# Moving strip copies ahead of the reading, a tanh between ScalarE's two gelu steps, and two bias additions from GpSimd to VectorE

## The chip, the cores and the metric

The kernel runs on one core of one Trainium2 chip. A core has five engines with an instruction stream each: TensorE (PE; its weight loads are listed as PEld), VectorE (DVE), ScalarE (ACT), GpSimd (POOL) and SyncE (SP), which issues most of the DMAs. [...] The metric is the device time of one execution in microseconds (us); a profiled execution has a span, from its first to its last recorded event, inside its own time.

## The reference, cut to what matters

`x` is 3327 x 64, `adj` a 3327 x 3327 matrix of zeros and ones, about 16 neighbours per row. Two layers follow each other, each added to `x`:

```
h = relu(layernorm(x))
x_t     = logmap0(h)                                   # c = 1 / r**2
adj_att = sigmoid(left[:, None] + right[None, :] + b) * adj
support = sum_j adj_att[i, j] * logmap(h[i], h[j])
x = x + proj(expmap(h, support))

h = relu(layernorm(x))
s = h @ weight
rank = cumsum(adj != 0, axis=1);  deg = rank[:, -1:];  k = min(deg, 100)
w = mask * where(rank - (deg - k) > 0, 0.5 ** (deg - rank), 0)
x = x + w @ s + bias
```

The first layer needs, for each pair of nodes, a function of three inner products; the second weights each neighbour by a power of two that depends on how many neighbours come behind it in its row.

## The kernel before, in words

**Tiling.** The nodes are padded to 26 blocks of 128. The columns i of the transposed `adj` are cut into four strips of 8, 8, 6 and 4 blocks (`STRIPS`); inside a strip the blocks j are taken from the last to the first. One *round* is one j in strips 0 to 2 and two j in strip 3, so that a tile is 128 x 1024, or 128 x 768 in strip 2. There are R = 91 rounds: 0 to 25, 26 to 51, 52 to 77 and 78 to 90. `js(n)` lists a round's blocks.

**One round.** For round n:

- `load` (L617): SyncE brings the 512 or 384 KB of `ad`, four rounds ahead, into one of five buffers.
- `edges` (L623): VectorE makes the 0/1 `mask`, two rounds ahead.
- `count` (L634, L635): TensorE counts neighbours behind each place into `pc`, of which there is one; one round ahead.
- `read` (L652 on ScalarE, L654 or L656 on VectorE): brings `pc` into the 8-bit or 16-bit store `behind`. `ON_ACT` says which share of the reads is ScalarE's: 1 of 2, 5 of 8, 3 of 4 and 1 of 2 by strip. The next `count` has to wait for it. In strip 3 a round has two counts and two reads, and the first read is VectorE's, the second ScalarE's.
- `products` (L680, L681): TensorE puts the pair's inner products in `pq`, one of two buffers in PSUM.
- `gelus` (L873, L874): ScalarE turns `pq` in place by two steps, the second of which takes what the first has written.
- `sigmoids` (L663): ScalarE writes tanh of the two nodes' logits into `sg`, one of five buffers, one round ahead; two instructions in strip 3.
- `pair_one` (L668): VectorE multiplies `sg` and `ad`.
- `pair_two` (L673): VectorE multiplies the result with `pq`, which is free then for the products two rounds on.
- `total` (L693): TensorE sums `sg` over j into the strip's two PSUM banks `po`, two rounds later.

**The order** on TensorE, VectorE and ScalarE is the program's (`manual_schedule(engines=IN_ORDER)`): the loop over n at L1244 writes it out by hand. GpSimd's and SyncE's order is the scheduler's. In the steady state of strips 0 to 2, ScalarE's order in round n is first step, second step, tanh of n+1, read (where it is ScalarE's); VectorE's is `pair_one(n)`, mask of n+2, read (where it is VectorE's), `pair_two(n)`; TensorE's is `total(n-2)`, count of n+1, products of n+1.

**The handover between strips.** Two rounds after a strip's last one, `strip_out` (L1170) copies the strip's sums out of `po`, the first 512 columns by VectorE (L1175), the rest by ScalarE (L1177). A round later `turn` (L1182) has TensorE transpose the copy (L1187) into the same banks, and `per_node` (L1190) copies that (L1197, L1199) and starts `post`: 64 features per node, for which VectorE does twelve larger operations, one per round in strips 1 and 2 and up to two per `advance` in strip 3, and GpSimd many small ones.

**The end.** With the last strip's sums the second layer starts: `decode` makes 16-bit weights of `behind` (L1336, L1339, L1340), `add` multiplies them with `s2` (L1237), and for each of four groups `copied` (L1378 to L1382) and `close` (L1384) bring the sums through one more matmul (L1390) and an addition with `x_sb` (L1392) to the output. `bias` (L1350) has GpSimd add the bias into `x_sb`, six times; two of these, for blocks 16 to 21 and 22 to 25, stand behind `finish()` in the program (L1366, L1367), and GpSimd ran them when `x_sb` was no longer needed unbiased, at 347.45 and 376.74.

Of the kernel before, what the change touches and what calls it, by code (L numbers as in the profile page):

```python
# [18 lines left out]
AF = mybir.ActivationFunctionType  # L19
# [4 lines left out]
P = 128  # L24
N = 3327
NB = 26
NP = NB * P
D = 64
K = D + 2
STRIPS = [(0, 8), (8, 8), (16, 6), (22, 4)]  # L30
# [42 lines left out]
QS = ZS * ZS / 2  # L73
WB = 936.0 / QS
WG = 4.885261340725196
WH = -0.0959413860521814
# [373 lines left out]
def fast(ctx, tc, x, adj_t, r, w_att, b_att, weight, bias, out, flag):  # L450

    nc = tc.nc
    V, A, G, T = nc.vector, nc.scalar, nc.gpsimd, nc.tensor
# [106 lines left out]
    R = len(rounds)  # L560
# [7 lines left out]
    ad_of, mask_of, sg_of, pq_of = {}, {}, {}, {}  # L568
# [31 lines left out]
    def part(n, t, j, a=0, b=None):  # L600
        k, lo, hi = rounds[n]
        F = strips[k].F
        return t[:, (j - lo) * F + a : (j - lo) * F + (F if b is None else b)]

    def span(n):
        k, lo, hi = rounds[n]
        return (hi - lo) * strips[k].F

    def js(n):
        k, lo, hi = rounds[n]  # L610
        return range(hi - 1, lo - 1, -1)
# [46 lines left out]
    def sigmoids(n):  # L658

        S = strips[rounds[n][0]]  # L660
        sg_of[n] = sg = work.tile([P, FMAX], F32, name="sg", bufs=SGB)
        for j in js(n):
            A.activation(part(n, sg, j), S.left[:, : S.F], AF.Tanh, bias=right[:, j : j + 1], scale=0.5)  # L663
# [62 lines left out]
    for hs in node_halves:  # L726
        n = hs.stop - hs.start
# [132 lines left out]
    bias_b = across(bias, D, "bias_b")  # L860
# [7 lines left out]
    A.copy(nz[:, high, 0], zf[:, high])  # L868
    V.tensor_copy(nu[:, high, :D], zf[:, high])

    def gelus(n):
        pq = pq_of[n][:, : span(n)]
        A.activation(pq, pq, AF.Gelu, scale=-WG / QS)  # L873
        A.activation(pq, pq, AF.Gelu, scale=WH)  # L874

    def logits(bs, plr=None):

# [28 lines left out]
    for b in (24, 20, 16, 12, 8, 4, 0):  # L906
        n = min(4, NB - b)
# [262 lines left out]
    def strip_out(k):  # L1170
        S = strips[k]
        S.ot = work.tile([P, FMAX], F32, name="sg", bufs=SGB)[: D + 1]
        for po, (f0, f1) in zip(S.po, S.hv):
            if f0 == 0:
                V.tensor_copy(S.ot[:, f0:f1], po[: D + 1, : f1 - f0])  # L1175
            else:
                A.copy(S.ot[:, f0:f1], po[: D + 1, : f1 - f0])  # L1177
# [49 lines left out]
    late = STRIPS[-1][0]  # L1227
# [16 lines left out]
    for n in range(2, R):  # L1244
        k, lo, hi = rounds[n]
        m, w = n + AHEAD, span(n)
        ended, turned = (n > i and rounds[n - i - 1][1] == 0 for i in (1, 2))
        if n + LOADS < R:
            if rounds[n + LOADS][2] == NB:
                strip_in(rounds[n + LOADS][0])  # L1250
            load(n + LOADS)
        fresh = EARLY <= m < R
        two = fresh and len(js(m)) == 2
        if two:
            count(m, js(m)[0])
        apart = k + 1 == len(STRIPS)
        if turned and not apart:
            pa = turn(k - 1)
        if n >= 4 and (apart or not turned):
            total(n - 2)  # L1260
        gelus(n)
        asked_of_act()
        if turned and not apart:
            finish()
            stages.append(Stage(per_node(k - 1, pa)))
        pair_one(n)
        if two:
            read(m, js(m)[0])
        if EARLY <= m + 1 < R:
            edges(m + 1)  # L1270
        if n == 2:
            for j in js(2):
                read(2, j, True)
        if n < 4:
            products(n + 1)
        if n == 2:
            total(1)
        if fresh:
            count(m, js(m)[-1])
        if n + 1 < R:  # L1280
            sigmoids(n + 1)
        if fresh:
            read(m, js(m)[-1])
        if 4 <= n < R - 1:
            products(n + 1)
        if ended:
            strip_out(k - 1)
        if hi - lo > 1:
            advance(PORTIONS[k])
        if turned and apart:  # L1290
            pa = turn(k - 1)
        pair_two(n)
        if turned and apart:
            finish()
            stages.append(Stage(per_node(k - 1, pa)))
        if n < 4:
            next(rest_of_ahead)
            continue
        advance(PORTIONS[k])
        if turned and not apart:  # L1300
            total(n - 2)
        if n >= R - len(JD):
            if n == R - len(JD):
                pw[0] = bank(0)
            add(JD[n - R], behind(JD[n - R]), 0)
        if n > R - 3:
            next(range_end)
# [15 lines left out]
    with tc.tile_pool(name="l1", bufs=2, reuse_waits="tile") as l1, tc.manual_schedule(engines=IN_ORDER):  # L1323
        decoded = 0

        def decode(j):

            nonlocal decoded
            if j in JD:
                return behind(j)  # L1330
            spare = decoded % (7 + len(JD)) - 7
            wt = weight_of[:, spare] if spare >= 0 else l1.tile([P, NP], U16, name="wt", bufs=7)
            decoded += 1
            to = by_parity(wt)
            if decoded * ACT_DECODES[0] % ACT_DECODES[1] < ACT_DECODES[0]:
                A.activation(to, behind(j).rearrange("p (k r) -> p r k", r=2), AF.Copy, scale=128.0)  # L1336
            else:
                pairs_of = behind(j).bitcast(U16)
                V.tensor_scalar(to[:, 0], pairs_of, 0xFF, 7, op0=ALU.bitwise_and, op1=ALU.logical_shift_left)  # L1339
                V.tensor_scalar(to[:, 1], pairs_of, 0xFF00, 1, op0=ALU.bitwise_and, op1=ALU.logical_shift_right)  # L1340
            return wt

        every = [*order, *range(late, NB)]
        weights = {j: decode(j) for j in every[: len(JD) + 1]}
        stages.append(Stage(per_node(len(STRIPS) - 1, pa)))
        pw[6] = ps.tile([P, FMAX], F32, name="pc")
        for n, j in beside:
            add(j, behind(j), n)

        def bias(b0, nb):  # L1350
            xb = x_sb[:, b0 : b0 + nb]
            G.tensor_add(xb, xb, bias_b[:, None, :].to_broadcast([P, nb, D]))  # L1352

        for i, j in enumerate(order):
            for jn in every[: i + 1 + LEAD]:
                if jn not in weights:
                    weights[jn] = decode(jn)
            asked_of_act()
            advance(LAST)
            for n in range(len(chunks)):  # L1360
                if j not in JD or n > 4:
                    add(j, weights[j], n)
            if i % 4 == 3 and i < STRIPS[-2][0]:
                bias(i - 3, 4)
        finish()
        bias(STRIPS[-2][0], late - STRIPS[-2][0])  # L1366
        bias(late, NB - late)  # L1367
        for j in range(late, NB):
            if j not in weights:
                weights[j] = decode(j)  # L1370
        kept_of = [l1.tile([P, min(NP - 1024 * q, 1024)], F32, name="ow" if q < 3 else "ow_last", bufs=2 if q < 3 else 1)
                   for q in range(4)]

        def copied(n):
            q, r = chunks[n]
            to = kept_of[q].rearrange("p (k r) -> p r k", r=2)
            if r is None:
                V.tensor_copy(to, by_parity(pw[n][:, :256]))  # L1378
            elif r == 0:
                V.tensor_copy(to[:, 0], pw[n])  # L1380
            else:
                A.copy(to[:, 1], pw[n])  # L1382

        def close(q):  # L1384
            for h in range(0, 8 if q < 3 else 2, 4):
                b0 = 8 * q + h
                nb = min(4, NB - b0)
                pc = pw[2 * q + h // 4]
                for b in range(nb):
                    T.matmul(pc[:, b * D : (b + 1) * D], kept_of[q][:, (h + b) * P : (h + b + 1) * P], w2s, start=True, stop=True)  # L1390
                o = l1.tile([P, 4, D], F32, name="o", bufs=4)
                V.tensor_add(o[:, :nb], pc[:, : nb * D].rearrange("p (b d) -> p b d", d=D), x_sb[:, b0 : b0 + nb])  # L1392
                full = nb if b0 + nb < NB else nb - 1
                f0 = b0 * P
                nc.sync.dma_start(out[f0 : f0 + full * P, :].rearrange("(b p) d -> p b d", p=P), o[:, :full])
                if full < nb:
                    nc.scalar.dma_start(out[f0 + full * P : N, :], o[: N - f0 - full * P, full])

        for n in range(len(chunks)):
            for j in range(late, NB):  # L1400
                add(j, weights[j], n)
            copied(n)
            if n > 0 and n % 2 == 0:
                close(n // 2 - 1)
        close(3)
# [52 lines left out]
```

## Time and profile before

| what | value |
|---|---|
| three runs | 404.16 us median (401.86 to 404.4) |
| the profiled execution's own time | 404.32 us |
| its span | 402.6 us, 4731 instructions |
| busy: PE, DVE, ACT, POOL | 355.0, 367.3, 355.3, 118.1 us (88, 91, 88, 29%) |
| L873, first step | 91 times, 958 ns mean; idle of ScalarE before it 1.1 us in all |
| L874, second step | 91 times, 947 ns mean; idle before it 2.9 us |
| L663, tanh | 103 times, 978 ns mean |
| L668 and L673, the two pair steps | 91 times each, 1144 and 1140 ns; VectorE's idle before L673 4.4 us, 3.8 of it for L874 |
| L1175, L1177, copies of the sums | 0.68 and 0.57 us for 512 columns |
| L1352, bias on GpSimd | 6 times, 1443 ns mean |
| waits of TensorE for L1175 | 2.6 us, twice, longest 1.7 |

A line of a timeline has the start in us from the span's start, the duration in us, engine, line, operation, the tiles written and read with their shapes, a count, and in brackets the engine's idle time just before it with the one it waited for. The durations of two neighbours can overlap on one engine: the next instruction starts before the last one's record has ended. So what an instruction costs its engine is read from start to start, and the duration is used for when its result is there.

### The profile page before, as it was taken

What the parts mean: (1) busy time and instruction counts of PE and PEld (TensorE: products, weight loads), DVE (VectorE), ACT (ScalarE), POOL (GpSimd) and SP (SyncE); (2) the same over time, 40 slices, a digit from 0 to 9 for tenths busy, and PEclk for the clock granted to TensorE, in tenths of its full rate; (3) what the DMA queues carried; (4) which work ended last, traced back from release to release, by engine and by line L of the source; (5) the groups of instructions that cost most, each with busy time, mean ns of one, the idle gap of its engine ahead of it and who ended that gap; (6) DMA issues with size and microseconds to landing.
All of it is one profiled execution on the core that took longest, in us unless ns stands there. A gap on an engine that the chain in (4) does not pass through costs nothing.

```text
span 402.6 us, 4731 instructions
## 1 busy us (share of the span) xinstructions
PE 355.0 (88%) x1460; PEld 151.9 (38%) x1460; DVE 367.3 (91%) x563; ACT 355.3 (88%) x407; POOL 118.1 (29%) x240
## 2 busy tenths in 40 slices
PE   0087999999999999999999899999979899999992
PEld 0063333333333333333333444444433233344462
DVE  4989999999999989999999999899999999898941
ACT  3589999999999999999999999999998999869510
POOL 8145200000000053870052052850240767241200
PEclk9999999999999899999999999999999999999997
DMA  7314555454548435553445545544563440000012
GB/s 202 150 42 133 171 157 158 128 165 138 163 139 237 148 106 156 156 157 109 153 116 148 149 120 157 131 134 128 152 188 117 111 152 0 0 2 1 2 42 52
DMA packets 23298, 48.99 MB, mean 122 GB/s; under 512 B 8789, under 2 KB 9245, under 8 KB 23265
## 3 DMA queue, kind: packets, MB, share of 16 engines
q1 hardware_dynamic: 20993, 47.66, 40.3%
q10 hardware_dynamic: 1808, 0.46, 0.6%
q0 software_dynamic: 464, 0.49, 0.5%
q8 instruction: 13, 0.21, 0.2%
q14 instruction: 20, 0.16, 0.1%
HBM read 46.40 MB, written 0.87 MB: 117 GB/s over the span
## 4 chain that ended last, share of the span: by engine, by line
DVE 32%; ACT 32%; PE 19%; issue 12%; DMA 1%; POOL 1%; POOLq 0%; DVEq 0%; ACTq 0%
ACT sg L663 11%; ACT pq L873 9%; DVE sg L673 8%; DVE sg L668 7%; PE po L693 7%; ACT behind_lo L652 3%; ACT pq L874 3%; PE pc L635 2%; PE pc L634 2%; PE pq L680 2%; PE pq L681 2%; ACT weight_of L652 2%; DVE behind_hi L656 2%; DVE mask L623 1%; ACT behind_hi L652 1%
## 5 line engine op out<-in xcount | busy, mean ns | idle before, releaser
L693 PE MATMUL po<-sg,hw 128*65 128x512 f32 (+1 forms) x364 | 159.5, 561 | 0.0
L673 DVE SCALAR_TENSOR_TENSOR sg<-pq,sg 128x1024 f32<-128x1024 f32 (+1 forms) x91 | 103.8, 1140 | 4.4 <-ACT pq L874 3.8
L668 DVE SCALAR_TENSOR_TENSOR sg<-sg,ad 128x1024 f32<-128x1024 f32 (+1 forms) x91 | 104.1, 1144 | 0.2
L663 ACT ACTIVATE sg<-left_b,right 128x1024 f32<-128x1024 f32 (+2 forms) x103 | 99.5, 978 | 0.0
L874 ACT ACTIVATE pq<-pq 128x1024 f32<-128x1024 f32 (+1 forms) x91 | 86.2, 947 | 2.9
L873 ACT ACTIVATE pq<-pq 128x1024 f32<-128x1024 f32 (+1 forms) x91 | 87.1, 958 | 1.1 <-PE pq L681 0.9
L693 PEld LDWEIGHTS po<-sg,hw 128*65 128x65 f32 x364 | 49.0, 137 | 67.3 <-issue 53.9
L634 PE MATMUL pc<-mask,ca 128*128 128x512 bf16 (+1 forms) x175 | 64.0, 366 | 10.1 <-ACT behind_hi L652 2.8
L680 PE MATMUL pq<-iu,ju 71*128 71x512 f16 (+1 forms) x182 | 67.5, 371 | 1.6 <-ACT jz L810 1.0
L635 PE MATMUL pc<-mask,cb 128*128 128x512 bf16 (+1 forms) x182 | 65.2, 369 | 1.8 <-ACT behind_lo L652 1.7
L681 PE MATMUL pq<-iz,jz 128*128 128x512 f16 (+1 forms) x182 | 65.9, 369 | 0.0
L623 DVE TENSOR_SCALAR mask<-ad 128x1024 bf16<-128x1024 f32 (+1 forms) x91 | 58.8, 647 | 0.0
L1062 POOL TENSOR_TENSOR dots<-dots,ih 128x8 f32<-128x8 f32 (+1 forms) x3 | 3.1, 1022 | 130.0 <-DVE dots L1082 130.0
L635 PEld LDWEIGHTS <-cb 128*128 128x128 bf16 x182 | 17.8, 98 | 51.8 <-issue 40.3
L634 PEld LDWEIGHTS <-ca 128*128 128x128 bf16 x175 | 17.2, 98 | 29.5 <-issue 17.3
L680 PEld LDWEIGHTS <-ju 71*128 71x128 f16 x182 | 17.9, 99 | 23.1 <-DVE sg L673 5.1
L1237 PEld LDWEIGHTS <-s 128*128 128x128 f16 x182 | 17.7, 98 | 20.2 <-issue 1.5
L681 PEld LDWEIGHTS <-jz 128*128 128x128 f16 x182 | 18.1, 99 | 19.1 <-issue 2.1
L652 ACT ACTIVATE behind_lo<-pc 128x1024 uint8<-128x1024 f32 (+2 forms) x29 | 24.9, 859 | 0.0
L1352 POOL TENSOR_TENSOR x_sb<-x_sb,bias_b 128x256 f32<-128x256 f32 (+1 forms) x6 | 8.6, 1443 | 51.7 <-DVE w L1151 46.0
L652 ACT ACTIVATE behind_hi<-pc 128x1024 uint8<-128x1024 f32 (+2 forms) x25 | 21.8, 871 | 1.2 <-PE pc L635 1.2
L844 PE MATMUL pq<-id,nui 128*71 128x128 f16 x8 | 1.0, 311 | 21.2 <-ACT nzi L818 21.2
(336 smaller groups left out, 396.0 us busy)
## 6 DMA issues: line engine op xcount, KB each, us to landing
ad<-in_adj_t SPq DMA_DIRECT2D x65, 512.0 KB, 3.6
ad<-in_adj_t SPq DMA_DIRECT2D x26, 384.0 KB, 3.1
out<-o SPq DMA_DIRECT2D x6, 128.0 KB, 1.9
left_b<-left_d SPq DMA_DIRECT2D x1, 512.0 KB, 5.0
x_sb<-in_x ACTq DMA_DIRECT2D x1, 416.0 KB, 5.7
x_sb<-in_x SPq DMA_DIRECT2D x1, 416.0 KB
left_b<-left_d SPq DMA_DIRECT2D x1, 384.0 KB
jz<-iz POOLq DMA_DIRECT2D x2, 128.0 KB, 2.6
```

What stands on the lines that cost most here:

```text
L623: V.tensor_scalar(*args, 0.0, None, op0=ALU.not_equal)
L634: T.matmul(S.pc[:, f0:f1], ca, S.before[:, f0:f1], start=False, stop=True, skip_group_check=True)
L635: T.matmul(S.pc[:, f0:f1], cb, now[:, f0:f1], start=S.first, stop=True, skip_group_check=True)
L652: A.activation(kept, of, AF.Relu, scale=128.0 if j in JD else 1.0)
L663: A.activation(part(n, sg, j), S.left[:, : S.F], AF.Tanh, bias=right[:, j : j + 1], scale=0.5)
L668: V.scalar_tensor_tensor(sg, sg, 1.0, ad_of.pop(n)[:, :w], op0=ALU.add, op1=ALU.mult)
L673: V.scalar_tensor_tensor(sg, pq_of.pop(n)[:, :w], WD, sg, op0=ALU.add, op1=ALU.mult)
L680: T.matmul(part(n, pq, j, f0, f1), ju[:KB, j, :], S.iu[:, f0:f1], start=True, stop=False)
L681: T.matmul(part(n, pq, j, f0, f1), jz[:, j, :], S.iz[:, f0:f1], start=False, stop=True)
L693: T.matmul(po[: D + 1, : f1 - f0], hw[:, j, :], part(n, sg_of[n], j, f0, f1), start=j == NB - 1, stop=j == 0)
L873: A.activation(pq, pq, AF.Gelu, scale=-WG / QS)
L874: A.activation(pq, pq, AF.Gelu, scale=WH)
```

## The change

- `gelus` is split into `gelu(n, scale)`. In rounds 4 to 89 (`n >= 4 and n + 1 < R`) the tanh of round n+1 stands between the two steps, rather than behind them; rounds 0 to 3 and the last keep the old order.
- `strip_out` of a finished strip comes before the tanh (where that is still at its old place) and before the round's last `read`, and no longer behind `products`.
- The last two additions of the bias are VectorE's, and stand behind the third of the seven `copied` of the end.

```diff
+    def gelu(n, scale):
+        pq = pq_of[n][:, : span(n)]
+        A.activation(pq, pq, AF.Gelu, scale=scale)
+
     def gelus(n):
-        pq = pq_of[n][:, : span(n)]
-        A.activation(pq, pq, AF.Gelu, scale=-WG / QS)
-        A.activation(pq, pq, AF.Gelu, scale=WH)
+        gelu(n, -WG / QS)
+        gelu(n, WH)
...
-        gelus(n)
+        tanh_first = n >= 4 and n + 1 < R
+        gelu(n, -WG / QS)
+        if tanh_first:
+            sigmoids(n + 1)
+        gelu(n, WH)
         asked_of_act()
...
         if fresh:
             count(m, js(m)[-1])
-        if n + 1 < R:
+        if ended:
+            strip_out(k - 1)
+        if n + 1 < R and not tanh_first:
             sigmoids(n + 1)
         if fresh:
             read(m, js(m)[-1])
         if 4 <= n < R - 1:
             products(n + 1)
-        if ended:
-            strip_out(k - 1)
...
-        def bias(b0, nb):
+        def bias(b0, nb, engine=G):
             xb = x_sb[:, b0 : b0 + nb]
-            G.tensor_add(xb, xb, bias_b[:, None, :].to_broadcast([P, nb, D]))
+            engine.tensor_add(xb, xb, bias_b[:, None, :].to_broadcast([P, nb, D]))
...
         finish()
-        bias(STRIPS[-2][0], late - STRIPS[-2][0])
-        bias(late, NB - late)
...
             copied(n)
+            if n == 2:
+                bias(STRIPS[-2][0], late - STRIPS[-2][0], V)
+                bias(late, NB - late, V)
             if n > 0 and n % 2 == 0:
                 close(n // 2 - 1)
```

## The prediction

> **What bounds the kernel now.** I read the page, then the busy time by stage, then the timelines of ScalarE, VectorE and TensorE side by side, and used the waits to see who is late. By stage (columns: length, then busy time of PE, PEld, DVE, ACT, POOL, granted clock, DMA share, GB/s):
>
> ```profile
> 47.00:127.00 80.00, 79.31 (x274) 29.89 (x273) 79.86 (x90) 79.27 (x81) 0.00 (x0) 1.00 0.52 155
> 127.00:145.00 18.00, 16.32 (x57) 6.32 (x56) 16.15 (x20) 16.70 (x20) 2.37 (x5) 0.91 0.54 156
> 235.00:276.00 41.00, 38.63 (x173) 18.50 (x172) 37.40 (x51) 40.56 (x55) 21.41 (x53) 1.00 0.48 135
> 297.00:326.00 29.00, 25.33 (x93) 9.77 (x91) 28.74 (x37) 27.24 (x40) 8.87 (x21) 1.00 0.45 130
> ```
>
> Strip 0 (to 127) has no slack anywhere: from start to start a round costs TensorE 3.45 us, VectorE 3.44, ScalarE 3.46. In strip 1 (to 223) a round of ScalarE costs 3.58 (two steps 1.97, tanh 1.04, a read 0.91 in five rounds of eight), TensorE's 3.45, and twelve rounds carry 0.6 more of VectorE. Strip 2 to 276 is ScalarE's: 40.56 of 41. From 276 to 326 VectorE never rests. The end of strip 3 is a loop through two engines (below). Strip 2, a round in which VectorE waits:
>
> ```profile
> 262.53 0.81 ACT L873 ACTIVATE pq<-pq 128x768 f32<-128x768 f32 x1
> 263.37 0.80 ACT L874 ACTIVATE pq<-pq 128x768 f32<-128x768 f32 x1
> 264.08 0.93 ACT L663 ACTIVATE sg<-left_b,right 128x768 f32<-128x768 f32 x1
> ...
> 264.20 0.96 DVE L673 SCALAR_TENSOR_TENSOR sg<-pq,sg 128x768 f32<-128x768 f32 x1 [0.75 <-ACT pq L874]
> ```
>
> The first step starts 0.84 before the second, which needs its result; the second starts only 0.71 before the tanh, which needs nothing of it. With 1024 columns the two are 1.05 and 0.92: the dependent pair wastes 0.13 us per round. L673 starts 0.83 after the second step (1.04 at 1024).
>
> **The skill.** "ScalarE: Activation LUTs", What ACT_TABLE_LOAD costs: an ACTIVATE with immediates takes 186 ns + 0.833 ns per column (1.04 and 0.83 us here; trace 1.01 and 0.80), and back-to-back ones overlap by about 93 ns. The trace agrees: 1.01 minus 0.92. It is this overlap that the dependent pair loses, plus 0.04. Alternating gelu and tanh loads no table: the trace's last load is at 21.56. "SBUF — State Buffer", SBUF: two separate sides: VectorE and GpSimd take a shared port pair as a lock, and the loser stands still (shown at the tail below). "TensorE: Matmul & The Clock Gate", What's actually happening: an idle TensorE falls to half clock after an idle window of about 3.4 us. The trace falls after 1.68, so I don't count on when.
>
> **Part 1, tanh between the steps.** By the condition on the round number this holds in rounds 4 to 89, all four strips, not only two; the changed program's order confirms it. Nothing is added; first step to tanh isn't in the old trace, so the gain lies between 0 and 0.13, and I take 0.13, since second step to tanh, the same shapes, is 0.92 everywhere. Two effects: ScalarE gains 0.13 per round, and the second step comes one tanh later (0.83 to 1.22), so L673 can too. VectorE runs in order: behind L673 stand L668, the mask and the read of the next round. Written sooner, a tanh needs its sum buffer sooner, one of five; the sum that frees it ran two rounds before, and at the handover about 0.8 ahead: free. I carry the old starts forward.
>
> - Start. The first step of round 4 is at 47.82; then tanh +0.92, second +1.04 = 49.78, L673 +1.04 = 50.82 against 50.10. VectorE has no gap in strip 0 to give it back: +0.7, also for TensorE, whose products in rounds 9 and 11 already wait for L673.
> - Strip 0 otherwise: TensorE's 3.45 stays. Zero; ScalarE merely moves up against the products (old slack 0.7 to 1.6).
> - Strip 1: VectorE's waits for others in rounds 37 to 39 (0.42, 0.50, 0.42) shrink to about 0.45 in all: -0.9. The rounds after carry an extra operation and are VectorE's: zero.
> - Strip 2: VectorE waits 0.66, 0.77, 0.20, 0.62, 0.75, 0.18, 0.17 between 249 and 276. Rounds 58 to 70 gain 12 x 0.13 = 1.5 (3 x 2.94 + 2.25 = 11.1 per four rounds against 11.66). From 276 on VectorE is full: zero.
> - Strip 3. Two reads per round, one by VectorE ahead of L673:
>
> ```profile
> 334.37 1.01 ACT L873 ACTIVATE pq<-pq 128x1024 f32<-128x1024 f32 x1
> 335.41 1.01 ACT L874 ACTIVATE pq<-pq 128x1024 f32<-128x1024 f32 x1
> 336.33 1.32 ACT L663 ACTIVATE sg<-left_b,right 128x512 f32<-128x512 f32 x2
> 337.56 0.58 ACT L652 ACTIVATE behind_lo<-pc 128x512 uint8<-128x512 f32 x1
> ```
>
> The old loop over two rounds: first step to read 3.19, read to the next-but-one first step through count, sum, count and products 4.29 (from 333.86 to 338.15): 7.48, or 3.74 a round. The 0.13 would make it 7.35. But a new loop opens: first step, tanhs 0.92, second step 1.22, L673 1.04, L668 1.14, VectorE's read 1.14, count 0.74, products 0.43, first step 1.07 = 7.70. That is 3.85 a round, where rounds 82 to 84 ran at 3.47. Its start costs too: round 78's first step is held by products at 298.17, its L673 moves from 300.33 to 301.35, +1.0. Carrying starts through rounds 79 to 90 with the extra operations, L673 of round 90 comes 2.6 later: +2.6 in all.
>
> **Part 2, copies ahead of the reading.** Same copies. VectorE's order changes only between strips 0 and 1, the other handovers having no VectorE read in that round; ScalarE's change at three.
>
> ```profile
> 129.79 1.22 DVE L656 TENSOR_SCALAR behind_hi<-pc 128x1024 uint8<-128x1024 f32 x1
> 130.92 0.68 DVE L1175 COPY sg<-po 65x512 f32<-65x512 f32 x1
> ...
> 130.94 0.57 ACT L1177 COPY sg<-po 65x512 f32<-65x512 f32 x1
> ...
> 131.65 0.81 PE L1187 MATMUL po<-ident,sg 65*128 65x65 f32 x8 [1.68 <-DVE sg L1175]
> 132.26 0.63 PE L634 MATMUL pc<-mask,ca 128*128 128x512 bf16 x1
> ```
>
> VectorE's copy moves up by one read, 1.13; ScalarE's by about as much against the products, having freed time. With the +0.7 in front, the transposes start near 131.2 and TensorE idles 0.7 rather than 1.7. After the old idle, eight matmuls start 0.43 apart instead of 0.216 (granted 0.91 of 18 us, 1.6 lost). Whether an idle of 0.7 costs the clock lies between 0 and 1.6; at 226.6 one of 0.9 cost none, so I take 0. VectorE later waited 1.85 at 143.6 for the count; without it, and with its 0.7 delay, L673 of round 30 comes at 143.5 against 144.76: -1.2 net of the start. If the clock still drops, -0.2. The read waits 0.6 behind the copy; its count is needed only by TensorE's next, which then has that room. Between strips 1 and 2 VectorE is the limit; I give nothing for the copy. Queues: TensorE's order is identical; SP's only swaps four small strip loads by one or two places, far ahead of use.
>
> **Part 3, last biases.** GpSimd drops two, VectorE gains 128x384 and 128x256 (0.48 and 0.34 by L1146's starts), after the third copy near 386. They delay output additions by about 0.5; those feed only stores, and VectorE next waits 1.23 for TensorE at 389: free. If that cover failed, +0.8. Gone is this:
>
> ```profile
> 376.74 1.01 POOL L1352 TENSOR_TENSOR x_sb<-x_sb,bias_b 128x256 f32<-128x256 f32 x1 [5.73 <-DVE w_last L1151]
> ...
> 377.08 1.12 DVE L1340 TENSOR_SCALAR weight_of<-behind_hi 128x1664 uint16<-128x1664 uint16 x1
> ...
> 382.75 0.61 PE L1237 MATMUL po<-weight_of,s 128*128 128x512 bf16 x2 [0.77 <-DVE s L1167]
> ```
>
> L1340 takes 0.59 elsewhere; the 0.53 lies on the path to L1167, for which TensorE waits 0.77: -0.5. Near 347.5 an L673 comes 0.17 late under the other bias: -0.2 (0 if chance). Locks elsewhere fall on other instructions now, up to 0.5 either way.
>
> **Sum.** Handover with start -1.2, strip 1 -0.9, strip 2 -1.5, strip 3 +2.6, tail -0.7: -1.7. The profiled execution took 404.32 (span 402.6 and 1.7 around it), so 402.6; the median of the runs is 404.16, 0.16 lower: **402.5**.
>
> **Rivals.** (a) The new loop of strip 3 doesn't bind (reads land sooner than 0.74): the +2.6 goes and the end gains 0.4: 404.2 - 4.7 = about 399.5. For it: VectorE has 0.35 in hand between 7.70 and the old loop. Against: each leg of 7.70 is a start-to-start from this trace. (b) Slower: the late second step holds L673 wherever a stretch of ScalarE's begins, because the first steps can't move up. Then VectorE loses 0.7 at the start, about 0.7 to 0.9 at each of rounds 29, 37 and 58, and 2.6 in strip 3, 5.8 in all; the tail gives 0.7, the freed 0.13s about 2.4: 404.2 + 2.7 = 406.9. It decides if old distances from products' end to first step, 0.5 to 1.9, shrink by less than about half. Against: that distance is ScalarE's own backlog. (c) The copies don't do what they should: the clock drops again after the transposes, so the handover gives 0.2, and VectorE then takes strip 1's gain: 404.2 - 0.2 - 1.5 + 2.6 - 0.7 = 404.4. For it: the old drop came after an idle of only 1.68.
>
> **Numbers.** As sketched 0.5 (own range 401 to 404), (a) 0.2, (b) 0.15, (c) 0.15. About 1% (4.0 us) is what a measurement here can tell from nothing: below 400.1 needs (a) nearly whole, 0.18; above 408.2 needs (b) with another loss, 0.06; the rest 0.76. The range runs from (a) to short of (b): 399.3 to 406.3.
>
> **What would show it.** First step to tanh 0.92 and tanh to second 1.04; VectorE idle 0.7 before round 4's L673; the transposes' wait under 1 us and 0.216 between matmuls after it; fewer VectorE waits between 249 and 276; rounds 82 to 88 near 3.85 with L673 waiting for the second step; L1340 uniform and no wait over 0.3 at the last L1237. I am wrong if strip 3 runs at 3.7 or less, or if waits for the second step appear throughout strips 0 and 1.

## The result, and the profile after

| | us |
|---|---|
| kernel before | 404.38 median (401.86 to 405.64, 14 runs) |
| kernel after | 404.15 median (403.24 to 405.71, 14 runs) |
| ratio | 1.0001, 95% interval 0.9984 to 1.0018 |
| profiled execution of after | 404.36, span 402.6 (before: 404.32, span 402.6) |

The forecast was 1.7 us less; nothing came. The same stages by busy time in after (columns as in the prediction: length, busy PE, PEld, DVE, ACT, POOL, granted clock, DMA share, GB/s):

```profile
127.00:145.00 18.00, 16.77 (x63) 6.42 (x62) 18.00 (x21) 17.31 (x21) 2.68 (x5) 1.00 0.50 148
235.00:276.00 41.00, 39.79 (x180) 19.13 (x179) 38.17 (x52) 41.00 (x57) 21.80 (x52) 1.00 0.52 145
297.00:326.00 29.00, 24.11 (x87) 9.18 (x86) 27.00 (x35) 26.19 (x39) 8.17 (x19) 1.00 0.40 116
326.00:349.00 23.00, 21.61 (x73) 7.80 (x72) 21.78 (x28) 21.16 (x28) 13.55 (x33) 1.00 0.13 41
```

At the handover (first row) the clock is 1.00 instead of 0.91, and VectorE has no gap. In strip 2 ScalarE is full, with 57 instructions where there were 55 in the same 41 us: it runs faster. In strip 3 (third row) VectorE rests 2.0 of 29 us, where it rested 0.26: a new wait. Two groups of the page name it (busy time and mean ns; then the engine's idle time just before, and what ended most of it). In after both steps stand in one line of the program, L873, and the lines behind it have numbers that are 3 higher than before:

```profile
L873 ACT ACTIVATE pq<-pq 128x1024 f32<-128x1024 f32 (+1 forms) x182 | 174.3, 964 | 5.3 <-PE pq L681 3.7
L673 DVE SCALAR_TENSOR_TENSOR sg<-pq,sg 128x1024 f32<-128x1024 f32 (+1 forms) x91 | 103.6, 1139 | 8.0 <-ACT pq L873 7.5
```

VectorE waits 7.5 us for the steps (3.8 before), and ScalarE 3.7 for the products.

To see where time is won and lost I keep a **ledger**: the start of L673 in each of the 91 rounds, minus its start in the first profile of before, with the difference at round 3 taken out. Rounds 0 to 3 run the old order in both kernels; their difference was 0.45 here, and -0.67 to 1.65 in five further profiles of before, so it varies with the execution. For after:

| stretch | forecast | measured |
|---|---|---|
| start, round 4 | +0.7 | +0.74 |
| handover, round 29 to 30 | -1.9 (-1.2 with the start) | -1.91 |
| strip 1, to round 51 | -0.9 | +0.03 |
| second handover, rounds 52 to 57 | 0 | -0.23 |
| strip 2, to round 77 | -1.5 | -1.08 |
| strip 3, round 78 and to 90 | +2.6 | +1.02 and +1.58 |
| tail | -0.7 | -0.58 |
| sum | -1.7 | -0.45 |

With the 0.45 of the start, the two spans are equal.

### The profile page after: what moved, and what is told of

The parts are those of the page before. It is cut to its first block, busy times and chain, and to the rows that moved or that the text cites. A ratio compares the mean times of both kernels' runs of the same rounds, so it can differ in the third digit from the quotient of the medians.

```text
span 402.6 us, 4731 instructions
## 1 busy us (share of the span) xinstructions
PE 354.4 (88%) x1460; PEld 151.1 (38%) x1460; DVE 367.3 (91%) x565; ACT 351.4 (87%) x407; POOL 117.0 (29%) x238
## 4 chain that ended last, share of the span: by engine, by line
DVE 40%; ACT 28%; PE 18%; issue 11%; DMA 1%; POOL 1%; POOLq 0%; DVEq 0%; ACTq 0%
ACT pq L873 15%; DVE sg L673 11%; DVE sg L668 10%; PE po L693 5%; ACT sg L663 5%; DVE behind_lo L656 4%; PE pq L680 2%; PE pq L681 2%; ACT behind_lo L652 2%; DVE behind_hi L656 2%; PE pc L634 2%; PE pc L635 2%; ACT behind_hi L652 2%; ACT weight_of L652 1%; DMA x_sb<-in_x 1%
## 5 line engine op out<-in xcount | busy, mean ns | idle before, releaser
L873 ACT ACTIVATE pq<-pq 128x1024 f32<-128x1024 f32 (+1 forms) x182 | 174.3, 964 | 5.3 <-PE pq L681 3.7
L693 PE MATMUL po<-sg,hw 128*65 128x512 f32 (+1 forms) x364 | 159.5, 561 | 0.0
L673 DVE SCALAR_TENSOR_TENSOR sg<-pq,sg 128x1024 f32<-128x1024 f32 (+1 forms) x91 | 103.6, 1139 | 8.0 <-ACT pq L873 7.5
L668 DVE SCALAR_TENSOR_TENSOR sg<-sg,ad 128x1024 f32<-128x1024 f32 (+1 forms) x91 | 103.8, 1141 | 0.1
L693 PEld LDWEIGHTS po<-sg,hw 128*65 128x65 f32 x364 | 48.9, 137 | 66.8 <-issue 53.5
L656 DVE TENSOR_SCALAR behind_lo<-pc 128x1024 uint8<-128x1024 f32 (+2 forms) x19 | 19.1, 1005 | 0.0
L1359 POOL TENSOR_TENSOR x_sb<-x_sb,bias_b 128x256 f32<-128x256 f32 x4 | 5.5, 1384 | 37.1 <-DVE w L1154 37.1
```

The costliest lines, as they stand in the source:

```text
L656: V.tensor_scalar(kept, S.pc[:, : S.F], 0.0, None, op0=ALU.max)
L668: V.scalar_tensor_tensor(sg, sg, 1.0, ad_of.pop(n)[:, :w], op0=ALU.add, op1=ALU.mult)
L673: V.scalar_tensor_tensor(sg, pq_of.pop(n)[:, :w], WD, sg, op0=ALU.add, op1=ALU.mult)
L693: T.matmul(po[: D + 1, : f1 - f0], hw[:, j, :], part(n, sg_of[n], j, f0, f1), start=j == NB - 1, stop=j == 0)
L873: A.activation(pq, pq, AF.Gelu, scale=scale)
```

## The experiments

Two theories stood against each other. Mine: the change is a sum of separate effects, a gain at the handover, one in strip 2, a loss where the order sets in and a large one in strip 3, and the missing time is in strip 1. The rival: the effects share one slack, so that parts of the change alone give what the whole gives, or the loss of strip 3 is not the new loop. Every kernel below is after with one edit, but for the repeated profiles. The ledger of all:

| kernel | 4 | 29 | 30 | 40 | 57 | 77 | 78 | 90 |
|---|---|---|---|---|---|---|---|---|
| after | 0.74 | 0.72 | -1.19 | -1.17 | -1.39 | -2.47 | -1.45 | 0.13 |
| after_2 (the same again) | 0.75 | 0.72 | -1.19 | -1.16 | -1.38 | -2.45 | -1.43 | 0.15 |
| bias_only | 0.01 | 0.00 | 0.02 | 0.02 | 0.02 | 0.00 | 0.00 | -0.01 |
| copies_only | 0.00 | 0.02 | -1.92 | -1.35 | -1.59 | -1.33 | -1.33 | -1.34 |
| no_tanh | 0.00 | 0.02 | -1.92 | -1.35 | -1.57 | -1.33 | -0.04 | 0.04 |
| tanh_strip0 | 0.75 | 0.72 | -1.20 | -1.20 | -1.44 | -1.18 | 0.10 | 0.18 |
| tanh_strip1 | 0.00 | 0.63 | -1.31 | -1.81 | -2.06 | -2.28 | -2.28 | -2.30 |
| tanh_strip2 | 0.01 | 0.03 | -1.91 | -1.35 | -1.38 | -2.41 | -2.41 | -2.42 |
| tanh_strip3 | 0.01 | 0.02 | -1.91 | -1.35 | -1.57 | -1.33 | -0.31 | 1.26 |
| tanh_half3 | 0.74 | 0.73 | -1.19 | -1.16 | -1.38 | -2.44 | -2.03 | -0.53 |
| tanh_strips12 | 0.01 | 0.64 | -1.30 | -1.81 | -2.02 | -3.10 | -3.10 | -3.10 |
| tanh_late12 | 0.00 | -0.01 | -1.94 | -1.35 | -1.57 | -2.64 | -2.64 | -2.64 |
| before_2, before_3 | 0.01 | 0.00, 0.03 | 0.02 | 0.01, 0.03 | 0.02, 0.06 | 0.01, 0.07 | 0.01, 0.07 | 0.02, 0.07 |
| before_4 | 0.00 | -0.03 | -1.66 | -1.41 | -1.41 | -1.45 | -0.18 | -0.17 |
| before_5 | 0.00 | 0.04 | -1.66 | -1.32 | -1.29 | -1.28 | -1.28 | -1.28 |
| before_6 | 0.01 | 0.03 | 0.03 | 0.03 | 0.06 | 0.07 | 0.07 | 0.08 |

**Without the tanh order: no_tanh.**

```diff
-        tanh_first = n >= 4 and n + 1 < R
+        tanh_first = n >= 4 and n + 1 < R and False
```

> Copies ahead and VectorE's biases kept, the tanh back behind both steps in all rounds. By the ledger of the two traces (each L673 against its old start) the handover between strips 0 and 1 gave 1.9 and the tail 0.6, and the tanh took 0.7 at the start, gave 1.2 in strip 2 and took 2.6 in strip 3. So this one should be about 2.5 under before: ratio 0.994. Rival: the engines are so balanced that what one stage gives comes back as a wait in the next, and the sum is near 1.000 here too.

402.48 us (22 runs), ratio to before 0.9967 (0.9949 to 0.9984): faster than after (1.0001; the two intervals meet at 0.9984), so the tanh order as a whole loses. It is less than the 0.994 that I expected, and not the rival's 1.000. The 1.3 us at round 78 are no part of the edit; copies_only, which differs only in the biases, hasn't them. They are the half clock of which before_4 tells below.

**The order in one strip at a time: tanh_strip0 to tanh_strip3.** The last condition of the same line is `k == 0`, `k == 1`, `k == 2` or `k == 3`.

> As no_tanh, with the tanh between the steps in strip 0 alone (rounds 4 to 25). Ledger: +0.7 at round 4 that VectorE and TensorE carry to the handover; there VectorE waits for TensorE, whose own chain decides: by the two traces round 30 came 0.74 before its old place with the 0.46 of a later beginning in it, so between 0 and +0.7 against no_tanh. Rival: strip 0 gains from the freed 0.1 a round: 2 us under no_tanh.

> As no_tanh, with the tanh between the steps in strip 1 alone (rounds 26 to 51). I had forecast -0.9 and the traces show 0: nine rounds of 0.1 freed are what one tanh of 0.94 in front of the second step takes. So no difference to no_tanh beyond 0.3. Rival: strip 1 loses or gains by itself and the changed kernel hid it under the handover: more than 0.7 either way.

> As no_tanh, with the tanh between the steps in strip 2 alone (rounds 52 to 77). Ledger: handover -1.9, tail -0.6, strip 2 -1.2, strip 3 as before: about -3.7, ratio 0.991. Round 78's L673 keeps its old distance to its first step. Rival: the gain of strip 2 is lost on the way into strip 3, where VectorE is full; then it equals no_tanh.

> As no_tanh, with the tanh between the steps in strip 3 alone (rounds 78 to 89). Ledger: -2.5 from handover and tail, +2.6 in strip 3: about 0, ratio 1.000; rounds 83 to 88 at 3.85, L673 of round 78 1.0 after its old distance. Rival: strip 3's loss in the changed kernel came from what it inherited from strip 2; then this equals no_tanh.

| kernel | median us | ratio to before | interval |
|---|---|---|---|
| tanh_strip0 | 402.32 | 0.9981 | 0.9958 to 1.0004 |
| tanh_strip1 | 402.57 | 0.9951 | 0.9932 to 0.997 |
| tanh_strip2 | 401.16 | 0.993 | 0.9906 to 0.9955 |
| tanh_strip3 | 404.89 | 1.004 | 1.0018 to 1.0062 |

The recorded ratio is not that of the two medians: tanh_strip0's 402.32 against 404.07 would give 0.9957. tanh_strip0 stays by the ledger within what I expected (0.15 behind copies_only at round 77), and tanh_strip2's ratio too. Two missed. tanh_strip1 is 0.49 ahead of copies_only at round 57 and 0.95 at round 77, where I had allowed 0.3. tanh_strip3 came to 1.004 instead of 1.000; of the 1.9 that I had counted for the handover 1.33 is left at round 77.

By the ledger strip 2 alone gives -1.0 (57 to 77) and strip 3 alone +2.6 (77 to 90), the same as in the whole: these two are independent of the rest. Strips 0 and 1 are not. Each pays 0.6 to 0.75 where its order sets in; but strip 1 alone then wins 0.50 between rounds 31 and 40, where after wins nothing, and without the order 0.57 is lost there.

**Half of strip 3's tanhs: tanh_half3.** Where the next round has two tanhs, only the first goes between the steps.

```diff
-            sigmoids(n + 1)
+            sigmoids(n + 1, 0, 1 if halved else None)
         gelu(n, WH)
+        if halved:
+            sigmoids(n + 1, 1)
```

> The changed kernel, but in strip 3 only the first of a round's two tanhs stands between the steps, the second behind both. If strip 3 loses by the loop first step, tanhs, second step, L673, L668, VectorE's read, count, products, first step (7.70 for two rounds), then 0.61 less in it makes it 7.1, less than the other loop's 7.4, and the rounds fall to about 3.7: of the 2.6 only 0.4 at round 78 stays, so about 2.2 under the changed kernel, ratio 0.994. Rival: the delay of the second step costs in proportion to its length; then half of 2.6 is lost, about -1.3, ratio 0.997.

403.28 us (22 runs), ratio 0.9982 (0.9966 to 0.9997). The entry (round 78) costs 0.41 instead of 1.02, one tanh of 0.61 less. I had expected 0.994; the rival's 0.997 is nearer, and of strip 3's 2.60 us 1.91 stay. But they don't stay as the rival has it. From round 85 the L673 (L675 in this kernel's own count) come 3.67 to 3.69 apart (332.41, 336.10, 339.78), no longer 3.85: the long loop is gone, and VectorE is full but for a wait of about 0.2 per round. From round 78 to 85 0.46 is lost, and from there to round 90 another 1.04, which has another cause:

```profile
342.16 0.56 DVE L1145 TENSOR_TENSOR w<-hw,of_end 128x384 f32<-128x384 f32 x1 [1.16 <-POOL of_end L1067]
```

VectorE has come to this step before GpSimd's chain of small operations is through; neither before nor after has that wait there.

**One of the other parts alone: copies_only, bias_only.** The first has neither the tanh order nor the moved biases, the second neither the tanh order nor the moved copies.

```diff
-        if ended:
-            strip_out(k - 1)
         if n + 1 < R and not tanh_first:
...
             products(n + 1)
+        if ended:
+            strip_out(k - 1)
```

(for bias_only; for copies_only the two `bias` calls are put back behind `finish()`.)

> The copies ahead of tanh and reading alone; biases on GpSimd and the tanh behind both steps as before. Ledger: the handover's 1.9, nothing else: ratio 0.995; TensorE's wait for the copy under 1 us and no half clock after it. Rival: the half clock after the transposes comes by chance and the copies gain only what VectorE waited beyond it: 0 to 0.5.

> VectorE's biases alone. Ledger: L1340's 0.53 at the tail and no more: -0.5, ratio 0.9987, just under what can be told from nothing; TensorE's last wait for L1167 0.2 rather than 0.77. Rival: GpSimd's bias was beside the path: 0.

copies_only 403.93 us (14 runs), ratio 1.0012 (0.9983 to 1.0042); bias_only 403.63 us (22 runs), 0.9987 (0.9967 to 1.0006). bias_only is as expected. copies_only is not: I had 0.995, and while the ledger gives the copies 1.34, the timed runs give nothing. That contradiction was not in my theory. Part of the answer is in the clock: bias_only, like before's first profile, shows half clock at the handover, and no kernel with the copies ahead does. Another part is the spread. Seven of copies_only's 14 runs took 402.31 to 402.94 us with a mean granted clock of 0.987 to 0.995, seven took 404.91 to 406.46 with 0.984 or 0.985. Its profile (402.66) is of the first kind. no_tanh's profile (404.75, 0.985) is of the second, and it has half clock twice, between 39 and 42 us and at the entry of strip 3; in the ledger it is behind copies_only by 1.70 at round 3 and by 1.29 more at round 78. That copies_only's seven later runs have the same is argued from their clock alone.

**More profiles of the two kernels: before_2 to before_6, after_2.** No edit.

> The kernel before once more, for a second execution. If the half clock of TensorE at the handover of strip 0 to strip 1 comes by execution, it is there or not, and the place is 0.9 us cheaper without it (the handover gain of the copies is then 1.0 instead of 1.9); other rounds stand as in the first profile within 0.05 us, but for the start (within 1.5).

> The kernel after once more. The ledger of second products by round repeats within 0.05 us but for the start and for the entries of strips, where TensorE's clock may halve or not: the loss in strip 3 is 2.6 again without a half clock there.

> Third execution of the kernel before. If TensorE's half clock after the 1.7 us pause at the handover comes only in some executions, a look without it shows round 30's second product 0.9 us earlier than the first profile (one theory: the copies' gain of 1.92 is half a shorter wait and half a clock that doesn't always fall); if it always comes, round 30 stands within 0.05 us of the first profile, and the spread of the timed runs comes from the start and from the entry of strip 3 alone (rounds 3 and 78: 0 or 1.3).

> Fourth execution of before, as the third: round 30 within 0.05 us of the first profile if the half clock at the handover always comes, 0.9 us earlier in a look without it.

> Fifth execution of before, as the third: round 30 within 0.05 us of the first profile if the half clock at the handover always comes, 0.9 us earlier in a look without it.

> Sixth execution of before, as the third: round 30 within 0.05 us of the first profile if the half clock at the handover always comes, 0.9 us earlier in a look without it.

404.63, 404.56, 403.49, 402.91, 405.98 us for before_2 to before_6, 405.22 us for after_2. TensorE at the handover, in the timeline of before_3:

```profile
131.73 0.71 PE L1187 MATMUL po<-ident,sg 65*128 65x65 f32 x8 [1.65 <-DVE sg L1175]
...
132.99 0.63 PE L635 MATMUL pc<-mask,cb 128*128 128x512 bf16 x1
133.41 0.63 PE L680 MATMUL pq<-iu,ju 71*128 71x512 f16 x1
133.84 0.63 PE L681 MATMUL pq<-iz,jz 128*128 128x512 f16 x1
```

and in that of before_5, the same kernel:

```profile
131.61 0.71 PE L1187 MATMUL po<-ident,sg 65*128 65x65 f32 x8 [1.65 <-DVE sg L1175]
...
132.80 0.38 PE L635 MATMUL pc<-mask,cb 128*128 128x512 bf16 x1
133.01 0.38 PE L680 MATMUL pq<-iu,ju 71*128 71x512 f16 x1
133.23 0.38 PE L681 MATMUL pq<-iz,jz 128*128 128x512 f16 x1
```

The pause is the same, 1.65 us. Once the matmuls behind it start 0.43 apart, once 0.216. Four of the six profiles of before (the first, 2, 3 and 6) have the half clock at this place and agree within 0.03 us at round 30; two (4 and 5) haven't it and stand 1.66 earlier. I had expected 0.9. So of the copies' 1.92 only 0.26 are left against an execution without the half clock, and by round 40 nothing of it: copies_only stands at -1.35, before_5 at -1.32.

The second place is in rounds 0 to 3, and it makes the largest differences of the start. The first profile of before, then before_6:

```profile
39.33 0.38 PE L634 MATMUL pc<-mask,ca 128*128 128x512 bf16 x1
39.59 0.38 PE L635 MATMUL pc<-mask,cb 128*128 128x512 bf16 x1
```

```profile
39.38 0.63 PE L634 MATMUL pc<-mask,ca 128*128 128x512 bf16 x1
39.81 0.63 PE L635 MATMUL pc<-mask,cb 128*128 128x512 bf16 x1
```

Between 39 and 42 us before_6, after_2, no_tanh and tanh_half3 were granted a clock of 0.54 to 0.56, the other 14 profiles 1.00. These four reach round 3 later than the first profile by 1.25 to 1.65, the others by -0.67 to 0.45.

The third place is the entry of strip 3. before_4, then tanh_strips12:

```profile
292.71 0.38 PE L635 MATMUL pc<-mask,cb 128*128 128x512 bf16 x1 [1.73 <-ACT behind_lo L652]
...
294.95 0.63 PE L634 MATMUL pc<-mask,ca 128*128 128x512 bf16 x1
```

```profile
291.21 0.39 PE L635 MATMUL pc<-mask,cb 128*128 128x512 bf16 x1 [1.23 <-DVE mask L623]
...
293.96 0.38 PE L680 MATMUL pq<-iu,ju 71*128 71x512 f16 x1
```

With the tanh order in strip 2 the pause is 1.23 instead of 1.73. After the longer one the clock halved in three of twelve profiles (before_4, no_tanh, tanh_strip0), for 1.27 us in before_4; after the shorter one in none of six.

**The order where it pays: tanh_strips12, tanh_late12.** The last condition is `k in (1, 2)`, or `(k == 2 or k == 1 and n >= 31)`.

> The kernel after, with tanh between ScalarE's two steps in strips 1 and 2 only (0 and 3 as before). If the parts add up as the single-strip runs suggest, VectorE's second product is 2.3 us ahead of the kernel before at the end of strip 1's effect (round 57: 2.06) and gains about 0.9 to 1.1 more in strip 2 (round 77: 3.0 to 3.3 ahead), nothing is lost in strip 3, and the tail gives 0.6: 400.3 us or so, ratio 0.990. The rival, that strip 2's gain is the same time as strip 1's (both only take the same slack out of VectorE's wait for ScalarE): 2.3 to 2.5 ahead at round 77, no better than strip 2 alone, ratio 0.993.

> The same, but tanh stands between the steps in strip 1 only from round 31 on, after the handover. If the loss of 0.6 to 0.7 where the order sets in is the price of one tanh ahead of a second step that VectorE already waits for, and the handover's wait absorbs nothing, then setting in after the handover loses less, because ScalarE is behind by then anyway or has slack: round 31 at 1.9 ahead, round 40 at 1.8 to 2.4, round 77 at 3.0 to 3.6, ratio 0.988 to 0.991. The rival: the loss of 0.7 comes wherever the order sets in, so that this is within 0.3 us of tanh_strips12.

401.26 us (7 runs), ratio 0.9926 (0.989 to 0.9962), and 401.24 us (7 runs), 0.9916 (0.9886 to 0.9945). Both beat before and after; they are not told apart from each other or from tanh_strip2. The ledger of tanh_strips12 (-3.10 at round 77) is tanh_strip1's -2.06 at round 57 and strip 2's -1.0 together. tanh_late12 missed: the loss comes where its order sets in, 0.70 in round 32 with a wait of 0.62 for the second step, instead of round 29. At round 40 it stands at -1.35, as without the order, and it ends at -2.64 where I had -3.0 to -3.6.

## Why the prediction was wrong

The ledger gives -0.45 where the forecast had -1.7. Of the 1.25 between them strip 1 makes 0.93 and strip 2 0.42; the rest is small and of both signs. The -0.45 itself can't be told from nothing in the timed runs, whose interval is about 0.7 us wide to either side.

**Start: right.** +0.74 against +0.7, in both profiles of after, in tanh_strip0 and in tanh_half3, and never given back in strip 0.

**Handover: right in size against the profile that it was made from, but two of six profiles of before haven't what it removes.** I had priced the lost clock at 1.6, and measured are 1.66. What I didn't ask is whether every execution pays it: it was in the one profile that I had. Against before_5 the whole ledger of after is 0.13 + 1.28 = 1.41 behind at round 90, and with the tail's 0.58, 0.8 slower; against the first profile it is 0.45 faster. The timed runs show no difference. Whether the change takes away before's best executions isn't shown. In the runs beside after, 1 of 14 of before and none of 14 of after lies below 403.2 us; in two other groups of before it is 18 of 63 and 25 of 66, so the share varies from group to group. Nor does a run's mean clock tell the handover: before_3, with the half clock there, and before_5, without it, both have 0.987.

**Strip 1: wrong, the step that failed.** "VectorE's waits for others in rounds 37 to 39 (0.42, 0.50, 0.42) shrink to about 0.45 in all: -0.9." (The third of them is before L673 of round 40.) In after they are 0.67 in round 37 and 0.60 in round 40, 1.27 in all, and the strip gave +0.03. The term failed in two ways.

First, it counts as if only VectorE's waits had to shrink. Between rounds 37 and 40 ScalarE sets the pace, and the handover, priced in another part of the forecast, had changed where the two stand. In no_tanh L673 of round 31 starts 1.93 earlier than in the first profile of before, but ScalarE's first step only 1.35. VectorE just waits longer, 0.82 in round 37 where it was 0.42, and by round 40 0.57 of the handover's gain is gone:

```profile
168.25 1.23 DVE L673 SCALAR_TENSOR_TENSOR sg<-pq,sg 128x1024 f32<-128x1024 f32 x1 [0.82 <-ACT pq L873]
```

Against that the order frees some 0.1 in each of the nine rounds from 31 to 40, and makes the second step one tanh, 0.94, later: +0.9 and -0.9. tanh_late12, whose order begins in round 31, stands at round 40 just where no_tanh does.

Second, the 0.7 of the start is paid again. TensorE carries it into the handover, as the forecast says, and there it meets a ScalarE that has moved up. TensorE in after, and behind it ScalarE:

```profile
131.71 0.71 PE L1190 MATMUL po<-ident,sg 65*128 65x65 f32 x8 [0.70 <-DVE sg L1178]
132.83 0.38 PE L634 MATMUL pc<-mask,ca 128*128 128x512 bf16 x1 [0.42 <-DVE behind_hi L656]
```

```profile
143.67 1.01 ACT L873 ACTIVATE pq<-pq 128x1024 f32<-128x1024 f32 x1 [0.42 <-PE pq L681]
```

ScalarE waits 0.28 for a count at 139.35 and 0.42 for products at 143.67. (The first profile of before has 0.87 and 0.30 at these two places, behind its half clock.) The read behind the copy, for which the forecast saw room, isn't what makes ScalarE wait: it does hold TensorE for 0.42, but it does so in copies_only, no_tanh and tanh_late12 too, and there ScalarE waits for nothing. copies_only:

```profile
131.25 0.38 PE L634 MATMUL pc<-mask,ca 128*128 128x512 bf16 x1 [0.42 <-DVE behind_hi L656]
```

What parts the kernels is strip 0. Of the eleven profiles with the copies ahead, ScalarE waits here in the four whose order begins in round 4 (after, after_2, tanh_half3 and, once, tanh_strip0) and in no other; with the start taken out, TensorE's long sum behind the handover (L693, x8) starts 0.74 later in after than in no_tanh. In tanh_strip1 ScalarE's second step of round 31 is 0.92 earlier than in the first profile of before, in after 0.28, and VectorE's wait in round 37 is 0.26; it is 0.67 in after (167.88):

```profile
166.46 1.23 DVE L673 SCALAR_TENSOR_TENSOR sg<-pq,sg 128x1024 f32<-128x1024 f32 x1 [0.26 <-ACT pq L873]
```

So the 0.50 that tanh_strip1 wins between rounds 31 and 40 goes with the start's 0.7. No run took that delay from TensorE alone.

**Strip 2: right mechanism, term too large.** I took 0.13 per round for a dependent pair parted by a tanh. ScalarE in after:

```profile
260.16 0.84 ACT L873 ACTIVATE pq<-pq 128x768 f32<-128x768 f32 x1
260.89 0.96 ACT L663 ACTIVATE sg<-left_b,right 128x768 f32<-128x768 f32 x1
261.71 0.84 ACT L873 ACTIVATE pq<-pq 128x768 f32<-128x768 f32 x1
262.44 0.84 ACT L652 ACTIVATE behind_lo<-pc 128x768 uint8<-128x768 f32 x1
```

From start to start 0.73, 0.82, 0.73, together 2.28 against 2.37 before (0.84, 0.71, 0.82). Each step costs 0.73 rather than the 0.71 that I carried over from the pair's second step. That is 0.09 per round, about 1.1 in twelve rounds, and 1.08 arrived.

**Strip 3: right.** Both terms, +1.0 at the entry and the loop of 7.70 per two rounds:

```profile
333.84 1.01 ACT L873 ACTIVATE pq<-pq 128x1024 f32<-128x1024 f32 x1 [0.26 <-PE pq L681]
334.76 1.32 ACT L663 ACTIVATE sg<-left_b,right 128x512 f32<-128x512 f32 x2
335.99 1.01 ACT L873 ACTIVATE pq<-pq 128x1024 f32<-128x1024 f32 x1
```

```profile
337.03 1.23 DVE L673 SCALAR_TENSOR_TENSOR sg<-pq,sg 128x1024 f32<-128x1024 f32 x1 [0.36 <-ACT pq L873]
```

First step 333.84, tanhs, second step 335.99, L673 at 337.03 with an idle wait; the next first step but one is at 341.54, 7.70 later, again held by the products. First steps held so stand at 318.44, 326.14, 333.84 and 341.54. tanh_strip3 loses the same 2.59 alone, tanh_half3 breaks the loop.

**Second handover: 0 forecast, -0.23.** It comes with the earlier copy (copies_only has -0.24 there as well) and is gone by round 58 without the tanh order.

**Tail: right, a little small.** The slow L1340 is uniform, and the last wait for `s` is short:

```profile
377.64 0.58 DVE L1347 TENSOR_SCALAR weight_of<-behind_hi 128x1664 uint16<-128x1664 uint16 x1
```

```profile
382.76 1.04 PE L1240 MATMUL po<-weight_of,s 128*128 128x512 bf16 x4 [0.21 <-DVE s L1170]
```

0.58 instead of 1.12, and a wait of 0.21 instead of 0.77: -0.5 as worked out. In all seven profiles with these biases on GpSimd the wait is 0.73 to 0.77, in all eleven with them on VectorE 0.18 to 0.21. The other 0.2, near 347.5, was not the bias's: L668 to L673 takes 1.31 there in after too. The timed gain of bias_only, 0.0013 of 404 or 0.5 us, fits, but its interval includes 1.

**The rivals.** (a), the loop doesn't bind: refuted by tanh_strip3 and tanh_half3. (b), a loss wherever ScalarE's stretches begin: seen once, where the order sets in (round 4, 29 or 32), and in strip 3; rounds 37 and 58 show little of it. (c), the clock drops again after the transposes: in none of the eleven profiles with the copies ahead.

## What to carry to other kernels

Moving an independent instruction between two dependent ones frees the engine a little per round (about 0.1 us here), and makes the second one's result late by the whole instruction put in (0.94): by these two numbers it pays where the engine that does it is the bound for more than about ten rounds, and it loses where the result closes a loop through other engines. Before pricing a lost clock from one profile, profile several executions of the same kernel: what one of them pays may be absent in the next. And when one term of a forecast moves an engine, the waits that a later term takes from the old trace have to be worked out anew.

## What the runs showed of the hardware

- At two places TensorE went to half clock after pauses of 1.65 to 1.75 us in 8 of 19 cases (5 of 7 at the handover, 3 of 12 at the entry of strip 3), the same kernel with the same pause sometimes and sometimes not. It cost 1.66 and 1.27 us of the span.
- The pause alone doesn't tell. After the pause of 1.42 us near 314 the clock fell in none of the 18 profiles, but between 39 and 42 us it fell in four of them, and there the longest pause in the 5 us before was 0.90 to 0.93 us. What decides stays open.
- Four profiles of before whose clock falls at the handover agree in each round's L673 within 0.08 us through 87 rounds. Differences of the whole time between them arise in rounds 0 to 3 alone, and the largest, 1.65, goes with a half clock there.
